# Values in pairs of chunks, sums in place, small steps on GpSimd, and a new order in a three-stage decoder block

## The chip, the cores and the metric

The kernel runs on one core of a Trainium2 chip. A time is device microseconds of one execution; the kernel's time is the median over several runs. Engines are called as in the profile: PE (TensorE), with PEld for its weight loads, DVE (VectorE), ACT (ScalarE), POOL (GpSimd), SP (SyncE, which here only issues DMAs).

## The reference

64 sequences ("batches" below) of 128 tokens with 512 features pass through three stages, each followed by a residual sum and a layernorm. All is float32.

```python
x = _layernorm(x + _L0_attn_ref(x, Wqkv, q_norm_w, k_norm_w, Wo))   # causal attention, 16 heads of 32, RMS norm and rope on q and k
x = _layernorm(x + _L0_xattn_ref(x, ctx, ctx))                      # 8 heads over the feature axis:
    # qh, kh, vh: [8, 16, 512]; qk = qh^T kh / sqrt(16) is [512, 512] a head; ret = softmax(qk) applied to vh
x = _layernorm(x + _L0_ffn_ref(x, weight))                          # x and weight rounded to fp8 and back in blocks of 128, then x @ weight.T
```

## The kernel before

The work is done batch by batch; several batches are in flight. For one batch there are these parts, with the names and lines used below:

- `self_attention`: load `x` (L409), transpose it on PE (L328), project with `wqkv` (L322, four float32 matmuls for each of q, k, v), RMS norm and rope (L429 to L441), scores in row-tiled matmuls (L462), mask, maximum, exponential (L472 to L480), scaling by 1/sum on POOL (L484), transposes, the outputs in column-tiled matmuls (L497), projection with `wo`, the sum with `x` into `h0` (L508), layernorm into `x1`.
- `split` and `stack`: q (from `x1`) and k (from the context `cx`) are split into three bf16 parts (L515 to L518), stored in DRAM (`d_q`, `d_k`, L521) and loaded again stacked (L550), so that one bf16 matmul over 96 rows gives a float32-like product. A batch has two halves of four heads (`s`), each with its `qs` and `ks` out of rings of three.
- `maxima` (L569): scores of two heads and one chunk of 128 columns, in a bank pair `mx`, of which DVE takes the negated maximum (L572). After the eight steps of a half, four small steps on DVE split the maxima in three bf16 parts `ns` (L579 to L582), PE transposes them (L586), ACT copies them (L588) and a DMA puts them in as three more rows of `qs` (L589).
- `scores` (L604): the same product in the other orientation, with the maxima subtracted by those three rows, in the bank pair `sc`; ACT takes the exponential (L607) into `e`, a ring of `NE` = 2 tiles, each one chunk of four heads. `maxima` runs `LEAD` = 12 steps ahead of `scores`.
- `values` (L618): for one chunk, four column-tiled float32 matmuls of `va` with `e`, summed over the four chunks of a half in the bank `av`. Each float32 matmul stands as two in the profile, so x8 is one chunk.
- `gather`, `cross_norm`: the result is copied (L336, `aw`), its row sums (`d_su`) and values (`ac`) are moved by DMA; the sums are loaded (L642, `rs`), inverted (L643), stored (L644) and loaded as a broadcast tile `rb` (L645); POOL scales `ac` (L647), DVE adds `x1` into `h1` (L649), layernorm gives `x2`.
- `ffn`: `quantize` rounds `x2` with the tiles `qy` and `qe` (L370 to L382, three of its steps on POOL), PE transposes (L388) and multiplies (L664), DVE scales into `ft` (L669), POOL adds up in `h1` (L671), layernorm gives `y` (L360), which is stored (L675).

The order of the instructions on each engine is not written out by hand. `Plan` collects all operations with their engine, an estimated cost and a due time, and `emit` places them one after the other: for each engine it takes the operation with the smallest `t + EAGER * at`, where `t` is its estimated start and `at` its due time, lowered to that of what depends on it. The due times come from the list `DUE`, one entry for each operation of a batch. `TURN` is the estimated price of a change between plain, row-tiled and column-tiled matmuls. What runs on SP, the loads and stores, is placed in the same way, and its queue works in that order. PSUM is shared out as `sc` (two banks), `mx` (two), `av` (one) and three banks `t` for everything else.

Of the kernel before, what the change touches and what calls it, by code (L numbers as in the profile page):

```python
# [8 lines left out]
F32 = mybir.dt.float32  # L9
# [7 lines left out]
P = 128  # L17
# [21 lines left out]
    -0.477, 6.406, 1.108, 8.738, -3.388, -1.975, 8.446, -3.211, 10.046, 7.308, 7.14, 6.348, 8.835, 8.498,  # L39
    0.443, 6.255, 8.093, 0.86, -0.351, 5.636, 7.136, 7.206, 8.857, 1.225, 8.516, 5.911, -2.993, 7.459, 8.982,  # L40
    6.702, 8.584, -5.195, 1.613, 9.25, -1.205, 8.309, 8.351, 8.7, -4.37, 6.314, 5.681, -1.329, 2.961, 0.446,
    4.994, 7.225, 7.441, 9.169, -4.195, -1.969, 6.862, 8.415, 6.701, 5.583, 6.848, -2.311, 5.936, 0.669,
    -4.336, -3.225, -0.65, 7.359, 5.273, 5.221, 6.697, 1.056, -0.699, 10.521, 7.725, 1.786, 9.317, -0.281,
    7.711, 9.842, 9.061, 1.577, 8.221, 8.006, 7.879, 8.309, -3.567, 8.595, -1.665, 7.728, 9.366, -2.72, 8.659,
    7.918, 8.136, 1.226, 7.377, 8.801, -1.9, -3.235, 7.155, 2.459, 8.078, -0.111, 7.922, -2.283, 5.744, 8.589,
    8.639, 8.798, 8.023, 8.345, -2.381, 6.687, -3.336, 7.068, 9.022, 8.525, 7.703, -3.294, 7.204, 7.939,
    6.409, 8.724, 7.655, 6.335, -1.792, 9.28, 6.159, 8.745, 9.751, 6.105, 6.091, 9.536, -2.089, -2.232, 9.199,
    0.309, 6.288, 7.752, -2.402, 7.063, 8.465, 7.427, 8.775, 8.582, 6.962, 6.325, 8.669, -0.787, -1.292,
    0.453, 0.296, 8.463, 7.71, 7.588, 7.733, 0.379, 6.155, 7.154, 4.889, 7.773, -0.595, 7.767, 9.666, -1.092,
    6.191, 6.563, 6.653, 9.013, 8.943, 0.439, -2.316, 7.671, 0.863, 7.589, 6.814, 9.034, 7.913, 8.909, 0.355,  # L50
    6.804, 8.655, -2.295, 8.48, 8.501, 6.94, 8.017, 6.906, 7.026, 8.43, -1.393, 6.234, 7.098, 1.585, 8.045,
    8.533, 0.468, 7.066, 8.861, 0.714, 8.882, 6.175, -1.35, 6.235, 7.375, 6.217, 8.925, 8.641, -1.356, 0.11,
    7.185, 9.58, 7.556, -0.724, 6.008, 0.98, 6.563, 0.096, -0.199, 6.617, 4.512, 7.397, 6.433, 1.976, 0.624,
    8.166, 0.903, 8.672, 6.633, 8.659, 7.036, 7.95, 5.571, 1.956, 8.387, 7.208, 1.108, 8.445, 5.939, 7.611,
    9.168, 10.789, 9.282, 9.545, 7.415, 7.227, 1.509, 9.523, 0.675, 8.502, 1.884, 5.826, 8.269, 5.729, 9.384,
    0.745, 8.88, 8.088, 6.299, 9.017, 6.601, 5.232,
]
NK, NX, NE, NT = 3, 4, 2, 1
# [18 lines left out]
class Plan:  # L77
# [7 lines left out]
    TURN = 0.14  # L85
# [5 lines left out]
    def op(self, engine, cost, emit, r=(), w=(), b=None, due=0.0, late=0.0, mode=0):  # L91
# [24 lines left out]
        if b is not None:  # L116
            i = self.count[b] = self.count.get(b, -1) + 1
            due = b + (DUE[i] if i < len(DUE) else due)
        self.ops.append((engine, cost, emit, due, late, banks, sorted(deps), (b, i), mode))

    def emit(self):
# [14 lines left out]
        for _ in ops:  # L136
# [4 lines left out]
            for e in ENGINES:  # L141
                mine = None
                for n in cand[e]:
                    if at[n] > limit and e != "SP":
                        continue
# [42 lines left out]
def decoder_kernel(  # L188
# [24 lines left out]
    nc.sync.dma_start(out=cst, in_=consts)  # L213
# [4 lines left out]
    for c in range(NC):  # L218
        nc.scalar.dma_start(out=wqkv[:, c, :], in_=w_qkv[c * P : (c + 1) * P, :])
    wo = cp.tile([P, NC, D], F32, name="wo")  # L220
    nc.scalar.dma_start(out=wo, in_=w_o.rearrange("(c p) n -> p c n", p=P))
# [3 lines left out]
    nc.scalar.copy(ident_h, ident)  # L225
# [11 lines left out]
    r_h = ring("h", 2, [P, D])  # L237
# [16 lines left out]
    r_rb = ring("rb", 1, [P, D])  # L254
# [3 lines left out]
    r_ft = ring("ft", 2, [P, D])  # L258
# [8 lines left out]

    banks = {
        "sc": [psp.tile([P, 2, D], F32, name="sc")],
        "mx": [psp.tile([P, 2, D], F32, name="mx")],  # L270
        "av": [psp.tile([P, D], F32, name="av")],
        "t": [psp.tile([P, D], F32, name=f"ps{i}") for i in range(3)],
    }

# [75 lines left out]
    def layernorm(h, kh, y, key, pr):  # L350
        s, k = small("ln")
        st, mv, ve = s[:, 0:6], s[:, 8:10], s[:, 10:11]
        op("DVE", 0.6, lambda: nc.vector.bn_stats(st, h), [kh], [k + "st"], pr)
        op("DVE", 0.08, lambda: nc.vector.bn_aggr(mv, st), [k + "st"], [k + "mv"], pr)
        op("DVE", 0.07, lambda: nc.vector.tensor_scalar_add(ve, mv[:, 1:2], LN_EPS), [k + "mv"], [k], pr)
        r, kr = rsqrt(ve, k, s, 12, pr)
        nb = s[:, 16:17]
        op("DVE", 0.08, lambda: nc.vector.tensor_scalar(nb, mv[:, 0:1], r, -1.0, ALU.mult, ALU.mult),
           [k + "mv", kr], [k + "nb"], pr)
        op("ACT", 0.5, lambda: nc.scalar.activation(y, h, AF.Identity, bias=nb, scale=r),  # L360
           [kh, k + "nb", kr], [key], pr)

    def quantize(src, key, pr):
# [4 lines left out]
        am, sc, rc = s[:, 0:NC], s[:, 8 : 8 + NC], s[:, 16 : 16 + NC]  # L368
        y, e, xq = r_qy[0], r_qe[0], r_xq[0]
        op("DVE", 0.6, lambda: nc.vector.tensor_reduce(am, s3, AX.X, ALU.max, apply_absolute_value=True),  # L370
           [key], [k], pr)
        op("DVE", 0.08, lambda: nc.vector.tensor_scalar_mul(sc, am, 1.0 / FP8_MAX), [k], [k + "sc"], pr)
        op("DVE", 0.08, lambda: nc.vector.reciprocal(rc, sc), [k + "sc"], [k + "rc"], pr)
        op("POOL", 0.97, lambda: nc.gpsimd.tensor_tensor(
# [6 lines left out]
        op("POOL", 1.2, lambda: nc.gpsimd.tensor_tensor(y, y, e, ALU.add), ["qy", "qe"], ["qy"], pr)  # L381
        op("POOL", 1.2, lambda: nc.gpsimd.tensor_tensor(xq, y, e, ALU.subtract), ["qy", "qe"], ["xq"], pr)  # L382
# [9 lines left out]
    def ffn_weights(o):  # L392

        wt, key = r_h[o % 2], f"h{o % 2}"
# [10 lines left out]
    def self_attention(b):  # L405
        at = lambda f: (b, f - 2.1)
        i2 = b % 2
        x_t, kx = r_x[i2], f"x{i2}"
        op("SP", 0.4, lambda: nc.sync.dma_start(out=x_t, in_=x[b]), [], [kx], at(-0.3), 5.0)  # L409
        xT, kxT = r_xT[i2], f"xT{i2}"  # L410
        tp = Bank("t", kxT)
# [3 lines left out]
        def project(j, pr, *then):  # L415
            ps = Bank("t", *then)
            matmuls(ps, pr, [(xT[:, c * P : (c + 1) * P], wqkv[:, c, j * D : (j + 1) * D]) for c in range(NC)],
                    [kxT])
            return ps

        for j in range(2):
# [7 lines left out]
            op("ACT", 0.7, lambda ps=ps, t1=t1, ss=ss: nc.scalar.activation(t1, ps.ap, AF.Square, accum_out=ss),  # L429
# [12 lines left out]
            op("POOL", 1.38, turn, [f"t1{j}", f"t2{j}"], [f"rot{j}"], pr)  # L442
            tp = Bank("t", f"hT{j}{i2}")
# [10 lines left out]
        for r0 in (0, 2):  # L454
            pr = at(0.35 + 0.1 * r0)
            two = [Bank("t", f"pr{(4 * b + r0 + n) % 3}") for n in range(2)]
# [8 lines left out]
            for n in range(2):  # L465
# [16 lines left out]
                op("ACT", 1.55, exps, [k], [kp, k + "su"], pr)  # L482
# [3 lines left out]
                tp = Bank("t", f"{kpT}{r}")  # L486
# [3 lines left out]
        o_ps = Bank("t", "oT")  # L490
# [12 lines left out]
        a_ps = Bank("t", "h0")  # L503
        pr = at(0.87)
        matmuls(a_ps, pr, [(oT[:, c, :], wo[:, c, :]) for c in range(NC)], ["oT"])
        h, kh = r_h[0], "h0"
        pr = at(0.95)
        op("DVE", 0.6, lambda: nc.vector.tensor_tensor(h, a_ps.ap, x_t, ALU.add), [a_ps, kx], [kh], pr)  # L508
        layernorm(h, kh, r_x1[b % NX], f"x1{b % NX}", pr)

    def split(u, b, src, key, pr):
# [3 lines left out]
        op("ACT", 0.48, lambda: nc.scalar.copy(sp[:, 0, :], src), [key], [f"sp0{n}"], pr)  # L515
        op("POOL", 1.1, lambda: nc.gpsimd.tensor_tensor(rt, src, sp[:, 0, :], ALU.subtract), [key, f"sp0{n}"], [f"rt{n}"], pr)
        op("ACT", 0.48, lambda: nc.scalar.copy(sp[:, 1, :], rt), [f"rt{n}"], [f"sp1{n}"], pr)  # L517
# [6 lines left out]
    def keys(b):  # L524
# [9 lines left out]
        op("ACT", 0.48, lambda: nc.scalar.copy(  # L534
# [22 lines left out]
    def maxima(j):  # L557
# [21 lines left out]
        op("DVE", 0.08, lambda: nc.vector.tensor_copy(ns[:, 0, :], x), kx, [f"ns{m}0"], pr)  # L579
        op("DVE", 0.08, lambda: nc.vector.tensor_tensor(x, x, ns[:, 0, :], ALU.subtract), [f"ns{m}0"], kx, pr)  # L580
        op("DVE", 0.08, lambda: nc.vector.tensor_copy(ns[:, 1, :], x), kx, [f"ns{m}1"], pr)
        op("DVE", 0.08, lambda: nc.vector.tensor_tensor(ns[:, 2, :], x, ns[:, 1, :], ALU.subtract),  # L582
# [27 lines left out]
    def values(s, c, av):  # L610
        b, g = divmod(s, 2)
        n = (4 * s + c) % NE
        e, va = r_e[n], r_va[b % 2]

        def go():
            for i in range(4):
                h = 4 * g + i
                nc.tensor.matmul(  # L618
                    av.ap[32 * i : 32 * i + 32, :], lhsT=va[:, c, 32 * h : 32 * h + 32], rhs=e[:, i, :],
                    start=(c == 0), stop=(c == NC - 1))  # L620
        op("PE", 0.83, go, [f"e{n}0", f"e{n}1", f"va{b % 2}"], [av], (b, g / 2 + (2 * c + 2) / 16), mode=COLS)
# [14 lines left out]
    def cross_norm(b):  # L636
        pr = (b, 1.15)
        n = b % 2
        x1, x2, ac, rs, rb = r_x1[b % NX], r_x2[b % 2], r_ac[n], r_rs[n], r_rb[0]
# [6 lines left out]
           [f"d_rs{n}"], ["rb"], pr, 5.0)  # L646
        op("POOL", 0.97, lambda: nc.gpsimd.tensor_tensor(ac, ac, rb, ALU.mult), ["rb"], [f"ac{n}0", f"ac{n}1"], pr)  # L647
        h, kh = r_h[1], "h1"
        op("DVE", 0.6, lambda: nc.vector.tensor_tensor(h, ac, x1, ALU.add),  # L649
           [f"ac{n}0", f"ac{n}1", f"x1{b % NX}"], [kh], pr)  # L650
        layernorm(h, kh, x2, f"x2{b % 2}", pr)

    def ffn(b):
        pr = (b, 1.35)
        x2, kx2 = r_x2[b % 2], f"x2{b % 2}"
        tp, half, sc, ks = quantize(x2, kx2, pr)
# [4 lines left out]
        h, kh = r_h[1], "h1"  # L661
        for c in range(NC):
            f_ps = Bank("t", f"ft{c % 2}")
# [4 lines left out]
            ft, kt = r_ft[c % 2], f"ft{c % 2}"  # L668
# [83 lines left out]
```

## Time and profile before

| | |
|---|---|
| median of 3 runs | 3017.85 us (3016.71 to 3019.81) |
| the profiled execution: its own time | 3015.46 us |
| the profiled execution: its span | 3013.7 us |
| granted PE clock, mean | 0.982 |
| DVE / ACT / POOL busy | 2590.2 / 2292.5 / 1402.5 us |
| DMA traffic | 249.97 MB, mean 83 GB/s |

The profile is one execution. Busy times are in us, a group's mean in ns. In a timeline row the first number is the start from the span's beginning, the second the length, then engine, line, operation, written tile <- read tiles, shape and count; in brackets stands how long the engine was idle before and what released it. The modelled end of a matmul reaches over the start of the next, since matmuls are pipelined; the distance from start to start is what a group takes.

### The profile page before, as it was taken

The numbers are of one execution on the slowest core, as the hardware profiler recorded it, in microseconds if no ns is written. First come the engines' busy times: TensorE is split into PE (matmuls) and PEld (weight loads), VectorE is DVE, ScalarE is ACT, GpSimd is POOL, SyncE is SP. The second block draws the span as 40 slices with busy tenths as digits, with TensorE's granted clock in tenths as the row PEclk, the third lists the DMA queues.
The fourth block names the chain that finished last, engine by engine and source line by source line (L and its number), as shares of the span: only waits on it lengthen the run. The fifth ranks groups of instructions, "written<-read, shape, count | busy, mean of one in ns | idle before, by whom it ended". The sixth has DMA issues, their size and how long they took to land.

```text
span 3013.7 us, 51770 instructions
## 1 busy us (share of the span) xinstructions
PE 2896.3 (96%) x16977; PEld 1304.4 (43%) x17040; DVE 2590.2 (86%) x5211; ACT 2292.5 (76%) x5382; POOL 1402.5 (47%) x1309
## 2 busy tenths in 40 slices
PE   7799999999999999999999999999999999999973
PEld 3334444444444444444444444444444444444420
DVE  3668888899899999889989989989988998998974
ACT  4467877777788787787787777878778778777853
POOL 3334454454445445444445444544544444544433
PEclk8899999999999999999999999999999999999996
DMA  3422322223223322232232232222222223223220
GB/s 119 61 81 80 91 82 82 91 83 86 83 85 87 87 86 83 83 90 79 85 90 83 85 86 85 85 85 87 84 85 88 81 83 91 82 83 90 79 59 26
DMA packets 162845, 249.97 MB, mean 83 GB/s; under 512 B 45328, under 2 KB 94608, under 8 KB 162448
## 3 DMA queue, kind: packets, MB, share of 16 engines
q1 hardware_dynamic: 161472, 242.47, 27.9%
q10 hardware_dynamic: 1104, 4.19, 0.4%
q8 instruction: 135, 2.21, 0.3%
q14 instruction: 134, 1.10, 0.1%
HBM read 159.01 MB, written 69.21 MB: 76 GB/s over the span
## 4 chain that ended last, share of the span: by engine, by line
PE 92%; DMA 2%; DVE 2%; ACT 1%; POOL 1%; issue 1%; SPq 0%; POOLq 0%; ACTq 0%; DVEq 0%
PE ps L322 28%; PE mx L569 16%; PE av L618 16%; PE sc L604 15%; PE ps L328 8%; PE ps L462 5%; PE ps L497 2%; PE ps L664 1%; DMA qs<-d_q 1%; PE ps L586 1%; DVE nm L572 1%; DMA x<-in_x_dram 1%; PE ps L388 1%; ACT e L607 0%; POOL h L671 0%
## 5 line engine op out<-in xcount | busy, mean ns | idle before, releaser
L572 DVE TENSOR_REDUCE nm<-mx 128x2 f32<-128x1024 f32 x1024 | 1251.2, 1222 | 248.1 <-PE mx L569 232.7
L607 ACT ACTIVATE e<-sc 128x1024 f32<-128x1024 f32 x1024 | 1047.4, 1023 | 504.3 <-PE sc L604 502.6
L322 PE MATMUL ps<-wqkv,xT 128*128 128x512 f32 x1536 | 759.7, 597 | 1.3 <-ACT xT L336 0.7
L569 PE MATMUL mx<-ks,qs 96*128 96x512 bf16 x2048 | 617.1, 382 | 34.4 <-DMA qs<-d_q 14.2
L604 PE MATMUL sc<-qs,ks 99*128 99x512 bf16 x2048 | 613.8, 380 | 9.0 <-ACT e L607 8.8
L484 POOL TENSOR_TENSOR pr<-pr,s_max 128x512 f32<-128x512 f32 x256 | 266.7, 1042 | 707.2 <-DVE s_max L483 692.4
L618 PE MATMUL av<-e,va 128*32 128x512 f32 x4096 | 539.5, 605 | 2.7 <-ACT e L607 2.4
L480 ACT ACTIVATE pr<-pr,s_max 128x128 f32<-128x128 f32 x1024 | 396.4, 392 | 6.8 <-DVE s_max L475 6.8
L569 PEld LDWEIGHTS <-qs 96*128 96x128 bf16 x2048 | 171.6, 98 | 510.3 <-issue 444.0
L322 PEld LDWEIGHTS ps<-wqkv,xT 128*128 128x128 f32 x1536 | 286.8, 191 | 177.3 <-issue 98.9
L604 PEld LDWEIGHTS <-ks 99*128 99x128 bf16 x2048 | 183.8, 97 | 336.6 <-issue 197.3
L441 POOL TENSOR_TENSOR rot<-t,t 128x256 f32<-128x256 f32 x256 | 184.9, 742 | 285.5 <-DVE t L435 177.8
L671 POOL TENSOR_TENSOR h<-h,ft 128x512 f32<-128x512 f32 x192 | 244.1, 1271 | 57.4 <-DVE ft L669 47.3
L322 PE MATMUL ps<-wo,oT 128*128 128x512 f32 x512 | 242.0, 594 | 0.0
L472 DVE TENSOR_TENSOR pr<-ps,cst 128x512 f32<-128x512 f32 x256 | 165.2, 686 | 41.0 <-PE ps L462 38.5
L669 DVE SCALAR_TENSOR_TENSOR ft<-ps,s_fp,ws 128x512 f32<-128x512 f32 x256 | 179.8, 743 | 23.1 <-PE ps L664 11.6
L480 ACT ACTIVATION_READ_ACCUMULATOR pr<-pr,s_max 128x1 f32 x1024 | 196.7, 192 | 0.0
L518 POOL TENSOR_TENSOR sp<-rt,sp 128x512 bf16<-128x512 f32 x128 | 148.5, 1160 | 95.0 <-ACT sp L517 94.1
L336 ACT COPY pT<-ps 128x512 f32<-128x512 f32 x256 | 144.0, 587 | 47.7 <-PE ps L328 47.2
L618 PEld LDWEIGHTS av<-e,va 128*32 128x32 f32 x4096 | 94.3, 108 | 179.4 <-issue 126.9
L475 DVE TENSOR_REDUCE s_max<-pr 128x4 f32<-128x512 f32 x256 | 166.3, 671 | 0.0
L328 PEld LDWEIGHTS ps<-cst,pr 128*128 128x128 f32 x1024 | 115.8, 142 | 107.8 <-POOL pr L484 73.4
(85 smaller groups left out, 3655.7 us busy)
## 6 DMA issues: line engine op xcount, KB each, us to landing
d_k<-sp SPq DMA_DIRECT2D x192, 128.0 KB
ks<-d_k SPq DMA_DIRECT2D x128, 192.0 KB
d_q<-sp SPq DMA_DIRECT2D x192, 128.0 KB
qs<-d_q SPq DMA_DIRECT2D x128, 192.0 KB
x<-in_x_dram SPq DMA_DIRECT2D x64, 256.0 KB
cx<-in_ctx_dram SPq DMA_DIRECT2D x64, 256.0 KB
ks<-d_k SPq DMA_DIRECT2D x128, 128.0 KB
qs<-d_q SPq DMA_DIRECT2D x128, 128.0 KB
```

The source lines that it names most:

```text
L322: op("PE", 0.86, lambda k=k, a=lhsT, b=rhs: nc.tensor.matmul(bank.ap, lhsT=a, rhs=b, start=(k == 0), stop=(k == len(parts) - 1)), r, [bank ...
L328: nc.tensor.transpose(bank.ap[:, c * P : (c + 1) * P], src[:, c * P : (c + 1) * P], ident)
L441: nc.gpsimd.tensor_tensor(vr[:, :, t, :], v1[:, :, t, :], v2[:, :, 1 - t, :], ALU.add)
L480: nc.scalar.activation(pc[:, c, :], pc[:, c, :], AF.Exp, bias=nm[:, c : c + 1], accum_out=su[:, c : c + 1])
L484: op("POOL", 0.97, lambda pc=pc, rs=rs: nc.gpsimd.tensor_tensor(pc, pc, rs[:, :, None].to_broadcast([P, NC, P]), ALU.mult), [k + "rs"], [k ...
L569: nc.tensor.matmul(M.ap[:, k, :], lhsT=qs[0:NSP, i, c * P : (c + 1) * P], rhs=ks[0:NSP, i, :], start=True, stop=True)
L572: op("DVE", 1.14, lambda: nc.vector.tensor_reduce(nm[:, 2 * p : 2 * p + 2, c], M.ap, AX.X, ALU.max, negate=True), [M], [f"nm{m}{c}{p}"], pr)
L604: nc.tensor.matmul(A.ap[:, k, :], lhsT=ks[0 : NSP + 3, i, c * P : (c + 1) * P], rhs=qs[0 : NSP + 3, i, :], start=True, stop=True)
L607: op("ACT", 0.92, lambda: nc.scalar.activation(e[:, 2 * p : 2 * p + 2, :], A.ap, AF.Exp, scale=scale), [A], [f"e{m}{p}"], pr)
L618: nc.tensor.matmul(av.ap[32 * i : 32 * i + 32, :], lhsT=va[:, c, 32 * h : 32 * h + 32], rhs=e[:, i, :], start=(c == 0), stop=(c == NC - 1))
L669: op("DVE", 0.65, lambda f_ps=f_ps, ft=ft, c=c: nc.vector.scalar_tensor_tensor(ft, f_ps.ap, sc[:, c : c + 1], ws[:, c, :], ALU.mult, ALU.m ...
L671: op("POOL", 1.2, lambda ft=ft, c=c: nc.gpsimd.tensor_tensor(h, h if c else x2, ft, ALU.add), [kt] if c else [kt, kx2], [kh], pr)
```

## The change

- `values` takes two chunks in one step, after every fourth score step instead of every second, and `NE` goes from 2 to 3.
- The tiles `h`, `rb` and `ft` go: the sums are formed in place in `x`, `ac` and `y`, `rb` is loaded into `qe`, and `ft` uses `qy` and `qe` in turn. The FFN weights are loaded through the `x2` tiles.
- To POOL: the four small steps on the maxima and the sum of `ac` and `x1`. To ACT: the scaling of the quantizer's maxima. For the last batch the quantizer's and FFN's POOL steps and those of `cross_norm` run on DVE.
- The first batch's self-attention uses the banks of `sc` and `av`, which are not needed yet; its `x` is the first load, and `wqkv` is loaded by thirds of columns instead of by row blocks.
- The planner's costs are changed, `TURN` goes from 0.14 to 0.1, operations whose banks are already allotted are exempt from its look-ahead limit, and the list `DUE` is replaced.

```diff
-    TURN = 0.14
+    TURN = 0.1
...
+        late += 0.05 * (engine == "PE")
...
-                    if at[n] > limit and e != "SP":
+                    if at[n] > limit and e != "SP" and all(k.slot is None for k in ops[n][5]):
...
-NK, NX, NE, NT = 3, 4, 2, 1
+NK, NX, NE, NT = 3, 4, 3, 1
...
+        "first": [sc[:, 0, :], sc[:, 1, :], av],
...
+    nc.sync.dma_start(out=r_x[0], in_=x[0])
+    nc.sync.dma_start(out=cst, in_=consts)
+    for j in range(3):
+        cols = slice(j * D, (j + 1) * D)
+        nc.scalar.dma_start(out=wqkv[:, :, cols], in_=w_qkv[:, cols].rearrange("(c p) n -> p c n", p=P))
...
-    def quantize(src, key, pr):
+    def quantize(src, key, pr, last=False):
...
+        eng, en = ("DVE", nc.vector) if last else ("POOL", nc.gpsimd)
...
-        op("DVE", 0.08, lambda: nc.vector.tensor_scalar_mul(sc, am, 1.0 / FP8_MAX), [k], [k + "sc"], pr)
+        op("ACT", 0.12, lambda: nc.scalar.mul(sc, am, 1.0 / FP8_MAX), [k], [k + "sc"], pr)
...
-        wt, key = r_h[o % 2], f"h{o % 2}"
+        wt, key = r_x2[o % 2], f"x2{o % 2}"
...
+        pool = "t" if b else "first"
...
-        op("DVE", 0.6, lambda: nc.vector.tensor_tensor(h, a_ps.ap, x_t, ALU.add), [a_ps, kx], [kh], pr)
-        layernorm(h, kh, r_x1[b % NX], f"x1{b % NX}", pr)
+        op("DVE", 0.6, lambda: nc.vector.tensor_tensor(x_t, a_ps.ap, x_t, ALU.add), [a_ps], [kx], pr)
+        layernorm(x_t, [kx], r_x1[b % NX], f"x1{b % NX}", pr)
...
-        op("DVE", 0.08, lambda: nc.vector.tensor_copy(ns[:, 0, :], x), kx, [f"ns{m}0"], pr)
+        op("POOL", 0.15, lambda: nc.gpsimd.tensor_copy(ns[:, 0, :], x), kx, [f"ns{m}0"], pr)
...
     def values(s, c, av):
...
+            for k, n in zip((c - 1, c), ns):
+                for i in range(4):
+                    h = 4 * g + i
+                    nc.tensor.matmul(
+                        av.ap[32 * i : 32 * i + 32, :], lhsT=va[:, k, 32 * h : 32 * h + 32], rhs=r_e[n][:, i, :],
+                        start=(k == 0), stop=(k == NC - 1))
...
-           [f"d_rs{n}"], ["rb"], pr, 5.0)
+           [f"d_rs{n}"], ["qe"], pr, 5.0)
...
+        op(eng, 0.6 if b == B - 1 else 1.23, lambda: en.tensor_tensor(ac, ac, x1, ALU.add), [f"x1{b % NX}"], ka, pr)
+        layernorm(ac, ka, x2, f"x2{b % 2}", pr)
...
-            ft, kt = r_ft[c % 2], f"ft{c % 2}"
+            ft, kt = ((r_qy, "qy"), (r_qe, "qe"))[c % 2]
...
+            op(eng, 0.6 if b == B - 1 else 1.23, lambda ft=ft, c=c: en.tensor_tensor(y, y if c else x2, ft, ALU.add),
+               [kt] if c else [kt, kx2], [ky], pr)
...
-        layernorm(h, kh, y, ky, pr)
+        layernorm(y, [ky], y, ky, pr)
...
-        if j % 2:
+        if j % 4 == 3:
             values(j // 8, j % 8 // 2, av)
```

## The prediction

> **What bounds the kernel now.** I read the page first: which engine fills the span, and where its slices are not full.
>
> ```profile
> PE 2896.3 (96%) x16977; PEld 1304.4 (43%) x17040; DVE 2590.2 (86%) x5211; ACT 2292.5 (76%) x5382; POOL 1402.5 (47%) x1309
> ```
>
> TensorE (PE) is busy for 96% of 3013.7 us. An average hides stages, so next the busy times in four stretches: start, steady run, last batches, tail. The columns are the stretch, its length, busy time of PE, of its weight loads, of DVE, ACT and POOL, the granted clock, DMA share and GB/s.
>
> ```profile
> 0.00:160.00 160.00, 117.52 (x533) 57.33 (x537) 83.61 (x170) 67.40 (x197) 52.54 (x63) 0.86 0.39 92
> 160.00:2860.00 2700.00, 2692.28 (x16030) 1221.58 (x16082) 2416.97 (x4860) 2154.80 (x5070) 1295.89 (x1202) 1.00 0.29 85
> 2860.00:2967.60 107.60, 81.59 (x405) 23.89 (x405) 71.19 (x135) 63.63 (x101) 35.63 (x30) 0.92 0.17 50
> 2967.60:3013.70 46.10, 4.87 (x15) 1.56 (x16) 18.39 (x49) 6.63 (x15) 18.46 (x15) 0.51 0.07 26
> ```
>
> In the steady 2700 us PE lacks 7.7 us: the time there is what PE's instructions take, in their order. The chain repeats every 44.55 us (wqkv matmuls at 1519.93 and 1564.47), one batch. The start leaves PE idle for 42.5 us, the last batches for 26.0, the tail for 41.2.
>
> A full engine gets faster only if its own work shrinks, so the third view is the timeline of PE in one batch (start, length, group). I read it from start to start.
>
> ```profile
> 1499.40 1.92 PE L618 MATMUL av<-e,va 128*32 128x512 f32 x16
> 1501.26 0.60 PE L604 MATMUL sc<-qs,ks 99*128 99x512 bf16 x2
> ...
> 1505.45 0.60 PE L604 MATMUL sc<-qs,ks 99*128 99x512 bf16 x2
> 1505.88 0.38 PE L664 MATMUL ps<-wT,fT 128*128 128x512 bf16 x1
> ...
> 1507.61 0.60 PE L604 MATMUL sc<-qs,ks 99*128 99x512 bf16 x2
> 1508.13 1.07 PE L618 MATMUL av<-e,va 128*32 128x512 f32 x8
> 1509.13 0.60 PE L569 MATMUL mx<-ks,qs 96*128 96x512 bf16 x2
> ...
> 1512.45 1.02 PE L322 MATMUL ps<-wqkv,xT 128*128 128x512 f32 x2
> 1513.50 0.59 PE L569 MATMUL mx<-ks,qs 96*128 96x512 bf16 x2
> ...
> 1532.86 1.07 PE L618 MATMUL av<-e,va 128*32 128x512 f32 x8
> 1533.74 1.06 PE L497 MATMUL ps<-pT,v 128*32 128x128 f32 x32
> 1534.61 1.04 PE L618 MATMUL av<-e,va 128*32 128x512 f32 x8
> ```
>
> A pair of score matmuls takes 0.43 us when a plain matmul follows (1505.45 to 1505.88), 0.52 when the column-tiled values (L618) follow: 0.09 to go in. One chunk of values takes 1.00 until the next plain matmul, two chunks back to back 1.86. So a chunk is 0.86 and the way out 0.14: **a visit to the column-tiled form costs 0.23 us beside its work.** Nine column-tiled steps a batch (eight chunks and the attention outputs, L497) lie in six visits: at 1508.13, 1510.57, 1514.46, 1517.72, 1532.86 (chunk, outputs, chunk) and 1543.95 (two chunks).
>
> The fourth view is the timeline of all engines in the tail.
>
> ```profile
> 2967.20 0.69 DVE L649 TENSOR_TENSOR h<-ac,x 128x512 f32<-128x512 f32 x1 [1.13 <-ACT y L360]
> 2967.65 0.59 ACT L336 COPY aw<-av 128x512 f32<-128x512 f32 x1 [0.49 <-PE av L618]
> 2976.34 0.65 SPq L645 DMA_DIRECT2D rb<-d_rs  x1
> 2985.40 1.27 POOL L647 TENSOR_TENSOR ac<-ac,rb 128x512 f32<-128x512 f32 x1
> 2989.03 0.69 DVE L649 TENSOR_TENSOR h<-ac,x 128x512 f32<-128x512 f32 x1 [0.98 <-ACT y L360]
> ```
>
> The second sum of batch 63 (L649) waits until layernorm of batch 62 has read `h1` (L360), because both use that tile. In the steady run it is the same: the scaling L647 runs at 1532.40, its sum one period after 1521.11, some 33 us later.
>
> **The change part by part.** *Values in pairs.* The same matmuls in four steps instead of eight. Two pairs can't touch: with three sets of exponentials, one set is left when a pair starts, and the second set of the next pair waits for it. So visits are four (outputs beside a pair) or five (outputs alone). Before, three of nine steps already lay beside another, outputs among them; I take four: 2 x 0.23 = 0.46 us a batch, over 63 batches 29 us. With five it is 14.5.
>
> *Work off DVE.* The four small steps on the maxima (21.5 + 22.4 + 23.3 + 21.9 us), the sum L649 (76.1) and a scaling (11.3) leave it: 176 us, or 2.8 of about 40 us a batch. DVE is not the bound (89.5% in the steady run), so this is worth only the PE stalls that its backlog causes. One shows above: the projection pair at 1512.45 takes 1.05 where 0.86 is usual, and the maxima matmul behind it needs a bank that a DVE reduce frees. 0.19 x 63 = 12 us at most from this; all stalls of that kind that I find are 0.33 a batch, 20 us; a new order can also add some, which I bound at 10. I take a gain of 6.
>
> *Work onto POOL and ACT.* The sum: 64 x 1.27 (row of L671) = 81 us. The 512 small steps: from 0.10 us (a memset of one element per partition) to 1.04 each (a 512-wide multiply); nearest is the memset of eight, 0.12, and with two inputs I take 0.25: 128 us. POOL goes from 1402 to about 1612, 53% of the span. ACT gains 64 x 0.21 = 13 us on 76%. Neither is near PE, so 0 for the time, while PE's fill covers it; the waits are rival three. The Trainium skill speaks against the moved sum (GPSIMD Engine Reference, section Engine selection: elementwise operations belong on VectorE, GpSimd is about twice as slow with two inputs); by it the sum would go from 0.69 to some 1.35 us. In this trace it took 0.68 at best on DVE but 1.19 in the mean, against 1.27 for its like on POOL, so little is lost; by either figure the total stays, since POOL has room.
>
> *Sums in place.* The tiles `h`, `rb` and `ft` go. The sum no longer waits for `h1`, which frees 33 us of lag. In return `rb` and half of `ft` live in the quantizer's `qe`. That makes a loop: the `rb` load at 1527.80, quantizing from 1538 to 1547, last addition at 1514.42 + 44.55 = 1559.0, so 31.2 us out of 44.55. It closes with 13 us to spare: 0. In-place `x` and `ac` are held for one layernorm longer, 4 us of rings of two batches: 0 while loads come more than that ahead; past that each us late would be paid per batch.
>
> *The tail.* Batch 63 works on DVE. Before: copy of the values 2967.65, `rb` issued at 2976.34 because the reciprocal stood behind a quantizer step at 2974.16, sum finished at 2989.72. After: `rs` issued at 2969.97, 2 us to land, `rb` at about 2973.8, 4.4 us to land (in the steady run 1527.80 to the multiply's start at 1532.40), two 0.69 operations: 2979.6, so -10. Quantizing with 0.69 instead of 1.04, 1.26, 1.26: -1.5; the additions 4 x (0.75 + 0.69) = 5.8 instead of 6.1. Best -12. If batch 62 still holds `qe` until 2985.44, `rb` lands at 2989.8 and this gain is gone; the loop through `qe` is then 3 us longer than that through `h1`, and the worst is +4. I take -8.
>
> *The start.* Batch 0's `x` is loaded first, wqkv comes by thirds, so the first projection needs 1 MB, not 3 (before, it waited for the last piece until 16.67 us and ended at 17.9): 0 to 8, I take 4. The FFN weights no longer wait for `h` tiles (PE stood for 4.06 at 82.29 behind them): 0 to 8, take 3. Batch 0's attention has three banks for itself; from 17.9 to its first `d_q` store at 64.2 it shared them with batch 1: 0 to 12, take 6; a worse order could lose 5. Together -13.
>
> **The sum**, against the profiled execution (3015.46 us, span 3013.7): -29 - 6 - 13 - 8 = -56, so 2959.5. The median of the runs is 2.4 above the profiled time: 2962.
>
> **The rivals.** *One: the order keeps five visits and nothing at the edges comes.* -14.5 and a few us: 2998 to 3008. For it: every order time is new, and the start depends on it. Against it: the trace holds a clear price per visit, and pairs can't be split.
>
> *Two: the turns are saved but come back as stalls*, since the longer step (1.86 us) delays the next score matmul, and ACT runs dry. ACT was idle between exponentials already (502.6 us waiting for scores), so PE has to stall on it 0.9 us a batch to eat 56 us: 3012 to 3023. Before, PE lost 8.8 us to exponentials in all.
>
> *Three, slower: the small steps stand behind POOL's waits.* POOL works in order and its multiply L484 waited for DVE 692.4 us in 184 waits, 3.8 each, up to 13.4. Queued behind them, the maxima reach their transpose late, then the transfer (L589) and the scores. For one half of the batch L589 is issued at 1503.80 and its first scores run at 1509.62; with about 2 us for the transfer (the small `d_su` store before took 1.7), 3.5 us are to spare. A delay of 4.5 us a batch pays back all gains; a wait of 5.5 (5.52 stands before L484 at 1529.28) costs 2.0 x 63 = 126 us, less 56: 3088. Against it: POOL is idle for half the time and an order can put the steps ahead of the multiply.
>
> **How the numbers follow.** Forecast 0.82, rival one 0.06, two 0.03, three 0.09. Faster by over 0.2% (6 us, about what a measurement of this kernel can tell from no change): 0.82 + 0.06 = 0.88; within it 0.03; slower 0.09. The best ends of all parts give -29 - 20 - 28 - 12 = -89, 2929. Five visits (-14.5) with no gain elsewhere gives 3003. Outside 2929 to 3003 lie rivals two and three and some of one.
>
> **What would show it.** Right: a period near 44.0 us, four visits with x16 of L618 each, PE still full between 160 and 2860, the copy of the last values to the end shorter by 8 us, DVE near 82%. Wrong: PE idle behind scores, or transposes (L586) behind POOL, in the steady run; five visits; a tail in which the `rb` load waits for the batch before.

## The result, and the profile after

The changed kernel takes 3028.99 us (median of 6 runs, 3027.45 to 3034.12); the kernel before, run beside it, 3017.28 us (6 runs, 3013.27 to 3019.81). The ratio is 1.0043, with a 95% interval of 1.003 to 1.0056: slower by 0.4%, where 1.8% faster was forecast. The profiled execution took 3034.12 us (span 3032.3), 5 us above its median.

First the page, busy times and the chain by engine.

```profile
PE 2906.4 (96%) x17040; PEld 1306.0 (43%) x17040; DVE 2457.1 (81%) x4576; ACT 2320.1 (77%) x5450; POOL 1565.7 (52%) x1876
...
PE 80%; DVE 13%; POOL 3%; DMA 2%; ACT 1%; issue 1%; SPq 0%; POOLq 0%; DVEq 0%; ACTq 0%
```

The chain before:

```profile
PE 92%; DMA 2%; DVE 2%; ACT 1%; POOL 1%; issue 1%; SPq 0%; POOLq 0%; ACTq 0%; DVEq 0%
```

VectorE (DVE) is relieved as forecast (81%), GpSimd (POOL) has about the load forecast (1565.7 us against 1612), TensorE (PE) is again 96% busy. Busy shares alone would not show a loss, but the chain does: DVE's part of it went from 2% to 13%. The same stretches as before (columns: stretch, length, busy PE, PEld, DVE, ACT, POOL, clock, DMA, GB/s):

```profile
0.00:160.00 160.00, 119.43 (x558) 59.15 (x559) 76.82 (x153) 70.35 (x205) 52.52 (x74) 0.87 0.34 82
160.00:2860.00 2700.00, 2683.83 (x15974) 1214.00 (x15972) 2277.64 (x4233) 2167.11 (x5095) 1450.21 (x1735) 1.00 0.28 85
2860.00:2988.90 128.90, 97.85 (x494) 31.25 (x493) 80.46 (x138) 74.94 (x135) 54.31 (x61) 0.87 0.19 57
2988.90:3032.30 43.40, 5.30 (x16) 1.56 (x16) 22.18 (x54) 7.70 (x18) 8.61 (x7) 0.53 0.08 28
```

PE lacks 16.2 us in the steady 2700, before 7.7. That is only the visible part, since the modelled end of a matmul covers most short waits. The timeline of PE in one batch, read from start to start, shows the rest.

```profile
1505.09 1.92 PE L625 MATMUL av<-e,va 128*32 128x512 f32 x16
1506.94 1.16 PE L469 MATMUL ps<-hT,hT 32*128 32x128 f32 x16
...
1508.47 0.60 PE L575 MATMUL mx<-ks,qs 96*128 96x512 bf16 x2
1509.00 0.24 PE L592 MATMUL ps<-ident_h,ns 128*48 128x128 bf16 x1
1509.17 1.13 PE L327 MATMUL ps<-wqkv,xT 128*128 128x512 f32 x2
1510.13 0.60 PE L610 MATMUL sc<-qs,ks 99*128 99x512 bf16 x2
...
1513.90 1.92 PE L625 MATMUL av<-e,va 128*32 128x512 f32 x16
...
1524.74 1.92 PE L625 MATMUL av<-e,va 128*32 128x512 f32 x16
...
1539.33 1.92 PE L625 MATMUL av<-e,va 128*32 128x512 f32 x16
1541.07 1.06 PE L504 MATMUL ps<-pT,v 128*32 128x128 f32 x32
```

Four visits to the column-tiled form a batch, the outputs (L504) beside one of them: just what was forecast. But the period is 44.86 us (these rows recur at 1549.95), not 44.0 and not the 44.55 of before. The span by stages, read from the starts of the copies that end each batch's values (L341, before L336): batch 2 at 264.22 us (before 263.81, +0.4), from there to batch 58 2512.70 us (2497.94, +14.8: 56 x 0.31 less some uneven batches of before), to batch 63 211.94 (205.91, +6.0), and from there to the end 43.48 (46.03, -2.6). Together +18.6, the difference of the two spans.

Two things stand in these rows. The transposes of the maxima's parts (L592), 48 columns wide, now stand alone among plain matmuls: 0.53 us from L575 to L592, 0.17 to the next, and that next pair of float32 matmuls takes 0.96 where 0.86 is usual. In the kernel before they stood here:

```profile
1501.70 0.60 PE L569 MATMUL mx<-ks,qs 96*128 96x512 bf16 x2
1502.23 0.24 PE L586 MATMUL ps<-ident_h,ns 128*48 128x128 bf16 x1
1502.40 1.16 PE L462 MATMUL ps<-hT,hT 32*128 32x128 f32 x16
...
1517.72 1.06 PE L618 MATMUL av<-e,va 128*32 128x512 f32 x8
1518.72 0.24 PE L586 MATMUL ps<-ident_h,ns 128*48 128x128 bf16 x1
1518.89 0.60 PE L604 MATMUL sc<-qs,ks 99*128 99x512 bf16 x2
```

One was wedged between a plain and a row-tiled step, the other behind a column-tiled one: both shared a change of form with a neighbour. Call an excursion any stretch of steps that aren't plain. Before has eight of them in a batch (six visits to the column-tiled form, two to the row-tiled L462) and after seven (four visits, of which one leads straight into L469, the other L469, and both L592 alone). One is saved, not two.

The second is a wait, here with all engines (brackets: idle before, releaser):

```profile
1536.26 1.23 DVE L578 TENSOR_REDUCE nm<-mx 128x2 f32<-128x1024 f32 x1
...
1536.68 0.19 ACT L487 ACTIVATION_READ_ACCUMULATOR pr<-pr,s_max 128x1 f32 x1
...
1537.40 0.17 DVE L490 RECIPROCAL s_max<-s_max 128x4 f32<-128x4 f32 x1
...
1537.65 1.04 POOL L491 TENSOR_TENSOR pr<-pr,s_max 128x512 f32<-128x512 f32 x1 [0.99 <-DVE s_rms L350]
...
1537.97 0.60 PE L610 MATMUL sc<-qs,ks 99*128 99x512 bf16 x2
...
1538.75 0.66 PE L333 MATMUL ps<-cst,pr 128*128 128x128 f32 x4 [0.18 <-POOL pr L491]
```

The sums of the exponentials are there at 1536.87, but the reciprocal stands behind a reduce that DVE began at 1536.26; POOL's scaling starts at 1537.65 and PE's transposes at 1538.75, 0.78 after the score pair ahead of them where 0.43 is usual. Other waits of 0.18 and 0.19 us stand ahead of L575 (at 1524.21 and 1537.54), for banks that the same reduces (L578) free; the first shows in PE's rows, 1.04 us from start to start where 0.86 is usual:

```profile
1523.17 1.02 PE L327 MATMUL ps<-wqkv,xT 128*128 128x512 f32 x2
1524.21 0.59 PE L575 MATMUL mx<-ks,qs 96*128 96x512 bf16 x2
```

Together these are 0.72 us a batch. Before, one wait of this kind (0.19) is shown above, and the prediction counted 0.33 in all, so I read 0.4 to 0.5 us a batch more.

### The profile page after: what moved, and what is told of

Read it like the earlier page. It is cut to its first block, busy times and chain, and to the rows that moved or that the text cites. A ratio compares the mean times of both kernels' runs of the same rounds, so it can differ in the third digit from the quotient of the medians.

```text
span 3032.3 us, 51753 instructions
## 1 busy us (share of the span) xinstructions
PE 2906.4 (96%) x17040; PEld 1306.0 (43%) x17040; DVE 2457.1 (81%) x4576; ACT 2320.1 (77%) x5450; POOL 1565.7 (52%) x1876
## 4 chain that ended last, share of the span: by engine, by line
PE 80%; DVE 13%; POOL 3%; DMA 2%; ACT 1%; issue 1%; SPq 0%; POOLq 0%; DVEq 0%; ACTq 0%
PE ps L327 22%; PE av L625 16%; PE mx L575 12%; PE sc L610 12%; PE ps L333 7%; DVE nm L578 5%; PE ps L469 5%; DVE pr L479 3%; DVE s_max L482 2%; POOL pr L491 2%; PE ps L672 2%; PE ps L504 2%; DVE s_ln L358 1%; PE ps L592 1%; DMA qs<-d_q 1%
## 5 line engine op out<-in xcount | busy, mean ns | idle before, releaser
L578 DVE TENSOR_REDUCE nm<-mx 128x2 f32<-128x1024 f32 x1024 | 1251.9, 1223 | 272.0 <-PE mx L575 255.8
L327 PE MATMUL ps<-wqkv,xT 128*128 128x512 f32 x1512 | 776.5, 603 | 0.0
L575 PE MATMUL mx<-ks,qs 96*128 96x512 bf16 x2048 | 615.4, 381 | 31.3 <-DVE nm L578 19.5
L625 PE MATMUL av<-e,va 128*32 128x512 f32 x4096 | 500.6, 607 | 0.2 <-ACT aw L341 0.2
L491 POOL TENSOR_TENSOR pr<-pr,s_max 128x512 f32<-128x512 f32 x256 | 266.2, 1040 | 285.2 <-DVE s_max L490 126.7
L575 PEld LDWEIGHTS <-qs 96*128 96x128 bf16 x2048 | 186.9, 98 | 391.9 <-issue 323.2
L327 PEld LDWEIGHTS ps<-wqkv,xT 128*128 128x128 f32 x1512 | 268.3, 191 | 126.1 <-issue 39.1
L585 POOL CAST ns<-nm 128x16 bf16<-128x16 f32 x128 | 25.4, 198 | 457.8 <-DVE nm L578 450.8
L625 PEld LDWEIGHTS av<-e,va 128*32 128x32 f32 x4096 | 108.2, 110 | 270.6 <-issue 269.6
L680 POOL TENSOR_TENSOR y<-y,qe 128x512 f32<-128x512 f32 x126 | 159.9, 1269 | 77.0 <-DVE qe L678 76.7
L333 PE MATMUL ps<-cst,pr 128*128 128x128 f32 x1008 | 161.7, 283 | 19.6 <-POOL pr L491 18.7
```

Of the source, the lines that this page charges most:

```text
L327: op("PE", 0.86, lambda k=k, a=lhsT, b=rhs: nc.tensor.matmul(bank.ap, lhsT=a, rhs=b, start=(k == 0), stop=(k == len(parts) - 1)), r, [bank ...
L333: nc.tensor.transpose(bank.ap[:, c * P : (c + 1) * P], src[:, c * P : (c + 1) * P], ident)
L491: op("POOL", 0.97, lambda pc=pc, rs=rs: nc.gpsimd.tensor_tensor(pc, pc, rs[:, :, None].to_broadcast([P, NC, P]), ALU.mult), [k + "rs"], [k ...
L575: nc.tensor.matmul(M.ap[:, k, :], lhsT=qs[0:NSP, i, c * P : (c + 1) * P], rhs=ks[0:NSP, i, :], start=True, stop=True)
L578: op("DVE", 1.14, lambda: nc.vector.tensor_reduce(nm[:, 2 * p : 2 * p + 2, c], M.ap, AX.X, ALU.max, negate=True), [M], [f"nm{m}{c}{p}"], pr)
L625: nc.tensor.matmul(av.ap[32 * i : 32 * i + 32, :], lhsT=va[:, k, 32 * h : 32 * h + 32], rhs=r_e[n][:, i, :], start=(k == 0), stop=(k == NC ...
```

## The experiments

Theory A: one excursion of 0.23 us was saved, not two, because the 48-wide transposes are a form too; and the new order has more just-in-time waits behind DVE's reduces and POOL's scaling than the saving is worth. Rival B: the four small steps on POOL delay the maxima. Rival C: the pairs themselves cost what they save. Rival D: the tile `qe`, wanted twice a batch, holds everything up. A period is the median distance between those copies over batches 3 to 57 of the profiled execution; after the change nearly every batch has it to 0.05 us, before it single batches are up to 0.4 longer.

**e1_ns_dve**: `nc.gpsimd` to `nc.vector` in the four small steps (L585 to L588), the order as it was planned for POOL.

> The kernel after, with the four small steps on the maxima issued on VectorE again, the order otherwise the same. Theory A (only one visit saved, and an order that leaves waits behind VectorE's reduces and GpSimd's scaling): the small steps on GpSimd aren't the cause. VectorE gets 512 x 0.17 us = 89 us back, 1.4 us a batch, and its reduces come no earlier: period 44.8 to 45.2 us against 44.86. Rival B (the steps on GpSimd delay the maxima's parts, or the scaling behind them): the scaling runs up to 1 us earlier, the 0.34 us wait for it is gone and the period falls to 44.5 us or below.

Measured: 45.39 us, one time of 3063.1 us. B is refuted: with the steps on DVE the batch is 0.53 us longer, and in the kernel after PE waits 0.2 us in all for POOL's small steps ahead of the 128 transposes (L592). What made the loss is one of the steps, the second cast (L587), and the transpose behind it waits 0.45 us in 62 batches:

```profile
1535.46 0.14 DVE L586 TENSOR_TENSOR nm<-nm,ns 128x16 f32<-128x16 f32 x1
1535.62 1.04 POOL L491 TENSOR_TENSOR pr<-pr,s_max 128x512 f32<-128x512 f32 x1 [2.29 <-DVE nm L586]
1535.64 1.05 DVE L587 CAST ns<-nm 128x16 bf16<-128x16 f32 x1
1536.08 0.60 PE L575 MATMUL mx<-ks,qs 96*128 96x512 bf16 x2
1536.91 0.16 DVE L588 TENSOR_TENSOR ns<-nm,ns 128x16 bf16<-128x16 f32 x1
1537.13 0.24 PE L592 MATMUL ps<-ident_h,ns 128*48 128x128 bf16 x1 [0.45 <-DVE ns L588]
```

The cast takes 1.05 us, exactly as long as POOL's scaling beside it. Of the 128 casts in this run 68 take 0.16 to 0.18 us, and none of these runs beside a POOL instruction; the other 60 take 1.05 to 1.12, and each of them runs beside a POOL instruction (59 times L491) and ends just after it. The loss is larger than I gave (0.34 at most); without these 0.45 it would be some 0.08, still not the gain that B asks for. A rule of the Trainium skill (GPSIMD Engine Reference, section Engine selection) gives elementwise work to VectorE. The lengths agree: the other three steps take 0.16 to 0.17 us on DVE against 0.20 to 0.22 on POOL. The time went the other way, because of what ran beside the cast. The sum on POOL and the scaling on ACT were not taken back by themselves.

**e2_split**: of each pair the first chunk one score step earlier.

```diff
-        if j % 4 == 3: values(pair)
+        part(c - 1) is issued ahead of score step j = 3 (mod 4), part(c) where the pair was
```

> The kernel after, but of each pair of chunks the first one's values run one score step earlier, by themselves: eight visits to the column-tiled form a batch and no step longer than 1 us, the order otherwise the same. Theory A (a visit costs 0.23 us, but only one was saved): four visits more, 4 x 0.23 = 0.92 us a batch, period 45.6 to 45.8 us, about 3087 us in all. Rival C (a pair of 1.85 us holds up the scores, which costs what the visits save): the waits go with the pairs, period 44.9 us or less, 3030 us or less.

Measured: 46.97 us; median 3163.71 us of 4 runs, ratio 1.0471 (1.0453 to 1.0488). C's figure is refuted, and by more than A asked: of the 2.11 us, four visits make 0.92 (a chunk alone again takes 1.00 until the next plain matmul). The remaining 1.2 I put down to waits, since an order planned for pairs meets split ones; of these I read 0.47, the transpose behind the small steps. So the size of this run says little; that the pairs do save is shown better by e10 and e11 below.

**e3_rb_own**: `rb = r_rb[0]`, a tile of its own.

> The kernel after, with a tile of its own for rb instead of the quantizer's qe, the order the same. Theory A: in the steady run the loop through qe has room, so the period stays at 44.86 us; in the tail rb of batch 63 is loaded as soon as its sums are stored (at 2995 instead of 3005.8), so the distance from the copy of the last values to the end falls from 43.5 us by 7 to 10, and the time by as much, to 3019 to 3022. Rival D (the tile qe, wanted twice in a batch, holds the steady run up): period 44.7 us or below and over 15 us less in all.

Measured: 44.87 us; median 3028.3 us of 7 runs, ratio 1.0033 (1.0022 to 1.0044). D is refuted. From the copy of the last values to the end 41.6 us instead of 43.5: 1.9 gained, not 7 to 10. My expectation was wrong here: the load was issued at 2992.68, early, but the multiplication stands in DVE's queue behind batch 62's layernorm, which waits for POOL's additions.

```profile
2992.68 0.65 SPq L655 DMA_DIRECT2D rb<-d_rs  x1
...
3001.89 0.69 DVE L359 BATCH_NORM_STATS2 s_ln<-y 128x6 f32<-128x512 f32 x1 [1.93 <-POOL y L681]
...
3003.68 0.68 DVE L657 TENSOR_TENSOR ac<-ac,rb 128x512 f32<-128x512 f32 x1
```

**e4_no_mult, e5_short_max, e6_both, e7_before_both**: the two suspected waits relaxed, one by one, together, and together in the kernel before.

```diff
-  nc.gpsimd.tensor_tensor(pc, pc, rs[...], ALU.mult)      # e4: nothing in its place
-  tensor_reduce(nm[...], M.ap, ...)                       # e5: M.ap[:, :, 0:384]
```

> The kernel after without GpSimd's scaling of the self-attention's exponentials by 1/sum, so they go unscaled into the transposes; everything else as it was. Theory A: the transposes no longer wait for that scaling, 0.34 us a batch where they did: period 44.45 to 44.6 us. If the time were set by the work of TensorE alone, or by the pairs (C): 44.8 to 44.9, since none of TensorE's work changes.

> The kernel after, but each reduce of the maxima reads 384 of its 512 columns, so it takes about 0.27 us less on VectorE; order and TensorE's work unchanged. Theory A: the waits of TensorE for the banks that these reduces free (0.18 + 0.18 + 0.19 us a batch) and the scaling behind the reduce go: period 44.2 to 44.5 us. Rival C (the pairs, or TensorE's own work, set 44.86): 44.8 to 44.9.

> The kernel after with both relaxed: no scaling of the self-attention's exponentials on GpSimd, and the short reduces. With the waits gone the period shows what TensorE's own work takes in this order. Theory A: 44.0 to 44.2 us. To be read against the kernel before with the same two edits: A (one visit saved) expects a difference of 0.15 to 0.3 us, the prediction's count (two visits) 0.46, and rival C (pairs save nothing) 0.

> The kernel before with the same two edits: no scaling on GpSimd, short reduces. Theory A: it had waits of 0.2 to 0.4 us a batch, so the period falls from 44.55 to 44.2 to 44.4 us, and e6 lies 0.15 to 0.3 below it. The prediction's count has 0.46 between the two, rival C none.

Measured: e4 44.41 (3002.52 us), e5 44.41 (3003.91), e6 44.17 (2985.32), e7 44.38 us (3000.26; one time each). A stands on each (e4 fell a little further than it gave). With none of PE's work changed, the kernel after falls by 0.69 us a batch and the kernel before by 0.17: the change added 0.52 of waits that these two edits remove. With the edits the change gains 44.38 - 44.17 = 0.21 us, about one excursion and not two. The loss of the steady run is then 0.52 - 0.21 = 0.31; this holds by construction, so the four periods split the loss and don't prove it a second time.

**e8_pad, e9_before_pad, e10_pad_both, e11_before_pad_both**: is the 48-wide transpose a form of its own? The tile is padded with zeros, so that the transpose is 128 wide.

```diff
-    r_ns = ring("ns", 2, [P, 3, 4 * NC], BF16)
+    r_ns = ring("ns", 2, [P, 8, 4 * NC], BF16)             # set to zero once
-    nc.tensor.transpose(half(), ns...)
+    nc.tensor.transpose(tp.ap.bitcast(BF16)[0:P, 0:P], ns...)
```

> The kernel after, with the tile ns of the maxima's parts padded with zeros from 48 to 128 columns, so that its transpose is 128 wide (of its output only the 48 rows are used); order unchanged. Theory A (the 48-wide transposes are a form of their own, and change of form is what they cost): both stand alone among plain matmuls, so each gives back 0.09 on the way in, about 0.06 of itself and 0.05 to 0.1 behind it, 0.45 us a batch; waits behind the scaling may take some of it: period 44.4 to 44.6 us, 3003 to 3016 us. Rival (their width is of no account): 44.86 as before.

> The kernel before with the same padding. Theory A: here one 48-wide transpose stood right behind a column-tiled step and the other right ahead of a row-tiled one, so they shared their changes of form with a neighbour and the padding saves only 0.06 to 0.07 each: period 44.4 to 44.5 us against 44.55. Rival (width is of no account): 44.55.

> The kernel after with the padding, without the scaling on GpSimd and with the short reduces, so without the waits. Theory A: 0.45 below the 44.17 of the same kernel without padding: 43.7 to 43.8 us, and 0.46 to 0.55 below the kernel before with the same three edits, which is the two visits of the prediction, that show only when the 48-wide form is out of the way. Rival: 44.17, and the difference to before stays 0.21.

> The kernel before with the padding, without the scaling on GpSimd and with the short reduces. Theory A: 0.1 to 0.15 below the 44.38 of the same kernel without padding: 44.2 to 44.3 us. Rival: 44.38.

Measured: e8 44.48 us, median 3007.09 us of 5 runs, ratio 0.9959 (0.9945 to 0.9973); e9 44.43 (one time, 3019.6); e10 43.71 (2955.11); e11 44.28 (2998.78). The four periods lie where A had them. In e8's timeline of PE the excursion is gone: 0.43 in, 0.06 for the transpose, 0.91 and 0.44 for the groups behind it.

```profile
1510.02 0.22 PE L592 MATMUL ps<-ident_h,ns 128*128 128x128 bf16 x1
1510.08 0.60 PE L333 MATMUL ps<-cst,pr 128*128 128x128 f32 x4
1510.52 1.02 PE L327 MATMUL ps<-wqkv,xT 128*128 128x512 f32 x2
...
1535.67 0.60 PE L575 MATMUL mx<-ks,qs 96*128 96x512 bf16 x2
1536.10 0.22 PE L592 MATMUL ps<-ident_h,ns 128*128 128x128 bf16 x1
1536.16 1.07 PE L327 MATMUL ps<-wqkv,xT 128*128 128x512 f32 x2
1537.07 0.60 PE L610 MATMUL sc<-qs,ks 99*128 99x512 bf16 x2
```

The same padding is worth 0.46 us a batch after the change (e6 to e10) and 0.10 before it (e7 to e11), and with it the two relaxed kernels differ by 0.57. That is the two visits of the prediction (0.46) and, as an estimate from PE's rows, 0.10 more: the row-tiled L469 that stands straight behind a pair pays no way in of its own (0.53 instead of 0.43 ahead of the L469 that stands alone). Taking the padding's 0.46 - 0.10 = 0.36 off again leaves the 0.21 of above. Both relaxed kernels still hold waits of some 0.2 us. Eighty columns of zeros turn the change from a loss into a gain of 0.4%.

**c1_order, d3_moved, d1_pad_moved**: can the order give the waits back with no work left out? c1 replaces the list `DUE` (and gives the planner the 48-wide transposes as a form and two other costs); d3 and d1 keep it and move operations past neighbours on their queues; all have a tile for `rb`, d1 the padding too.

> The kernel after with a tile of its own for rb and another list DUE (searched with the durations of the trace after, the 48-wide transposes counted as a form of their own); the instructions are the same, only their order differs. Theory A: the loss was in the order, so a looser one brings the saved visit to light: period 44.2 to 44.5 us, time 2995 to 3012. Rival C (pairs cost as much as they save in any order): 44.7 us or more, 3020 or more.

> The kernel after with a tile of its own for rb and, for batches 3 to 58, operations moved past neighbours on their engines' queues after the planner is done (moves chosen by a model of the queues with the durations of the trace after). Theory A (the order leaves waits of 0.5 to 0.7 us a batch): they can be had back in part without leaving work out: period 44.35 to 44.6 us, time 2998 to 3015. If the waits belong to the change itself and not to its order: 44.8 or more, 3025 or more.

> The kernel after with the padded transpose, a tile of its own for rb and moves of the same kind. Theory A: the padded kernel has 44.48 - 43.71 = 0.77 us of waits a batch, of which the moves take about 0.3: period 44.1 to 44.3 us, time 2984 to 2998. If the waits can't be moved away: 44.5, 3005.

Measured: c1 47.8 us a batch, uneven between 39 and 59, median 3305.89 us of 4 runs, ratio 1.0963 (1.0945 to 1.0982): a failure of my order, in which the chain runs through transfers that come late.

```profile
1245.32 7.05 DMA d_rs<-rs
1252.44 4.27 DMA rb<-d_rs
...
1270.20 8.07 DMA cx<-in_ctx_dram
```

It tells of that list, not of A. d3: 44.49 us, median 3018.27 us of 12 runs, ratio 0.9987 (0.9978 to 0.9996): the same instructions as after with e3's tile, 0.38 us a batch less by order alone, enough to pass the kernel before by 0.1%. Its time missed the range that I gave (3015 at most): batch 2's copy comes at 270.77 us instead of 264.22, and batches 55 to 58, where the moves stop, take up to 49.21 us. d1: 44.48 us, median 3010.16 us of 6 runs, ratio 0.9958 (0.9946 to 0.9971): the period missed (44.1 to 44.3), no better than e8. Moves in a padded kernel trade one wait for another, so how much of its 0.77 us an order could save stays open.

**e12_rows, e14_pad_rows_rb, e15_pad_rows_rb_short**: the edges, and a version that beats both kernels.

```diff
-    for j in range(3): load wqkv[:, :, thirds of columns]
+    for c in range(NC): load wqkv[:, c, :]                 # e12, e14, e15, with e8's padding and e3's tile in the last two
```

> The kernel after with wqkv loaded by four row blocks again; x still first, order the same. If loading by thirds gave nothing (all loads share the engines that move them, and the first third landed at 12.8 us): first projection from about 10 to 13 us and done at about 18, first scores within 1 us of 112.4, period 44.86. If thirds did bring the 4 us forecast: the first scores come 3 to 5 us later.

> The kernel after with the padded transpose, wqkv by row blocks and a tile of its own for rb, order unchanged. If the three gains add: period 44.48 us, first scores at 108.6 instead of 112.4, tail 1.9 us shorter, so 5 to 6 us below the padded kernel: 0.994 of the time before, 3000 to 3004 us. If the start's gain is waited away in the first batches: 0.9955 to 0.996.

> The same with the reduces of the maxima over 384 of 512 columns (the softmax is the same with any shift that keeps the exponentials in range, so only the shift changes). If the waits behind VectorE's reduces were 0.45 us a batch as without the padding: period 44.0 to 44.1 us, another 24 to 28 us less: 0.985 to 0.987 of the time before. If the wait for the scaling only takes their place: 44.3 us or more, 0.99 or above.

Measured: e12 first projection at 12.55 us, done at 16.9 instead of 18.1, first scores at 108.61, period 44.87, 3028.35 us: earlier than after, which neither side had. That end is not shown to be the load's: in e12 the projection's matmuls stand 0.85 us apart up to 16.02 and 0.43 behind it, in after 0.85 up to 18.13. And e14 has its first scores at 112.82 again, with a projection that starts at 14.46, and padded e8, with thirds, had them at 109.75. The start varies by 4 us between kernels that load alike, so rows or thirds can't be told apart. e14: 44.48 us, median 3006.8 us of 5 runs, ratio 0.9952 (0.994 to 0.9964), between the two that I gave, and its interval reaches both. e15: 43.95 us, median 2968.56 us of 5 runs, ratio 0.9823 (0.981 to 0.9837), better than expected: the shorter reduces on DVE are worth 0.52 us a batch with the scaling left in. e15 is the fastest here, 1.8% below before; its softmax is shifted by the maximum over three quarters of the columns, so its range of safe inputs is smaller. With full maxima e14, d1 and e8 are the fastest; their intervals overlap.

## Why the prediction was wrong

- **Turns, -29 us.** Price right (0.23 us a visit; e2's rows repeat it), column-tiled visits right (six to four). The failed step is the count: it took "visits to the column-tiled form" for all changes of form. The rows of before already showed one 48-wide transpose with 0.53 ahead of it and the other behind a column-tiled step, each sharing its change with a neighbour. Measured: 0.21 us a batch, 13 us over 63, and 0.57 a batch with the transposes out of the way.
- **Work off DVE, -6 us.** The largest error. The working allowed 10 us for stalls that a new order might add and put DVE's relief against it; the change added 0.52 x 63 = 33 us of waits, of which another order of the same instructions gave back 0.38 a batch (d3). DVE's busy share fell to 81%, and PE's waits behind it rose: in the rows above what counts is whether a reduce is begun just ahead of the short step that PE waits for. "A full engine gets faster only if its own work shrinks" was right; that PE would stay full was assumed.
- **Work onto POOL, 0.** Held: 1.28 us for the sum (forecast 1.27), 0.20 to 0.22 for the small steps (forecast 0.25), 1565.7 us in all (forecast 1612). Rival three's queue did not form in the steady run: PE waited 0.2 us in all for the small steps. How long the transfer behind them (L595) takes is not shown.
- **Sums in place, 0.** Held in the steady run (e3).
- **Tail, -8 us.** -2.6 from the last copy to the end. The case named as the worst for `rb` came about: its load waits for batch 62's last addition, though `d_rs` had been stored ten microseconds before.

```profile
2995.18 0.33 SPq L653 DMA_DIRECT2D d_rs<-rs  x1
...
3004.54 1.26 POOL L680 TENSOR_TENSOR y<-y,qe 128x512 f32<-128x512 f32 x1
3005.83 0.64 SPq L654 DMA_DIRECT2D qe<-d_rs  x1
...
3009.48 0.69 DVE L656 TENSOR_TENSOR ac<-ac,qe 128x512 f32<-128x512 f32 x1 [1.77 <-DMA qe<-d_rs]
```

  Freeing the tile in the same order gives 1.9 more (e3), since DVE's queue has the same batch 62 ahead of it. In d3 and d1, which have that tile and whose operations were moved up to batch 58, the same distance is 35.4 us, 10.6 below before. But there batches 59 to 63 take longer (219.2 and 215.2 us; after 211.9), so that from batch 58's copy to the end d3 takes 254.5 us and d1 250.6, after 255.4 and before 251.9. That the 8 us could be had as a whole is not shown.
- **Start, -13 us.** +0.4 by batch 2 (batch 0's last copy came 3.5 us earlier, batch 1's took it back). `x` was transposed at 7.16 us instead of 10.68, but the projection began at 12.88, after 4.64 us of waiting for its third of `wqkv`, against 12.44 before. The 4 us for the thirds rested on a misreading. The wait that ended at 16.67 in the kernel before was one of PE's weight loads and held no matmul up: the projection runs without a gap from 12.44, its matmuls 0.85 us apart up to 16.00 and 0.43 from there on, past 16.67 too.

```profile
12.44 8.02 PE L322 MATMUL ps<-wqkv,xT 128*128 128x512 f32 x14 [0.68 <-ACT xT L336]
...
16.67 0.39 PEld L322 LDWEIGHTS ps<-wqkv,xT 128*128 128x128 f32 x2 [0.47 <-DMA wqkv<-in_L_attn_Wqkv_dram]
```

  In place of the wait of 4.06 us behind the FFN weights PE now waits 7.21 ahead of 71.55, for POOL's scaling (L491). Why the freed banks brought nothing stays open. How much of the start was gained is uncertain too, since one execution differs from the next: e3, with the same order, has batch 2's copy at 259.40, 4.4 us ahead of before, and e12 at 257.64.
- **The last batches.** Not in the sum at all: batches 59 to 63 take 6.0 us longer, of which the period makes 1.6. The rest is open. In this stretch the granted clock is 0.92 where it was 0.96 before; whether that or their order made it is not shown.
- **The sum.** Steady run and last batches +20.8 in place of -35, start +0.4 in place of -13, tail -2.6 in place of -8: +18.6 in place of -56. The medians differ by less, 11.7, since this profiled execution is 5 us above its median and that of before 2 below; e3 suggests that the 5 lie in the start. Rival two came nearest (turns come back as stalls, 0.03), but with another mechanism: the stalls are not at exponentials for want of scores, but at the transposes and maxima behind DVE. That it came near is luck.

## What to carry to other kernels

Before counting what a fused step saves, list every neighbour that shares its change of form, small transposes included; moving one step away can leave another paying alone. In a kernel whose bound engine is 99% full in its order, a new order is a change of its own: price it by relaxing the suspected waits in both kernels, not by the busy shares of the other engines. A reduce of 1.2 us begun just ahead of a 0.17 us step on the same queue costs the bound engine more than the load suggests. And when a short step is moved to another engine, look at what runs beside it there (e1), not only at the queue.

## What the runs showed of the hardware

In these kernels a bf16 transpose of 48 columns costs about what a change of tiling costs: 0.53 us in, 0.17 for itself and 0.05 to 0.1 on the float32 matmuls behind it, against 0.43, 0.06 and 0 to 0.05 for one padded to 128 columns; the wider one is faster, by 0.46 us for two (e6 to e10). The Trainium skill (TensorEngine Tiling (Array Packing), section Key Properties) states that a change of tiling mode drains TensorE. The runs put 0.23 us on a visit to the column-tiled form and back, and as much on one of these transposes standing alone; that it is a drain, and the same one in both, no run here shows. A cast of 128x16 (L587) takes 0.20 us on POOL; on DVE (e1) it takes 0.16 to 0.18 alone and 1.05 to 1.12 beside POOL's multiply or sum of 128x512, just after whose end it ends.
